# ScalarE's instructions in the order in which the work is given out, and counts widened up to five blocks ahead: a two-layer graph network on one core

## The chip, the cores and the metric

One core of a Trainium2 chip runs the whole program. It has a matmul engine (TensorE, PE in the rows; PEld is its loading of the stationary operand), three engines for elementwise work (VectorE or DVE, ScalarE or ACT, GpSimdE or POOL), an engine that only issues transfers (SyncE or SP), and 16 DMA engines that move data between the main memory and the on-chip memories. Matmul results land in a small memory with banks (tiles whose names end in `_ps`), from which ScalarE or VectorE copies them. Each engine runs its own list of instructions strictly in its order; where an instruction needs another engine's result, it waits, and all that stands behind it on its engine waits with it. The metric is the device time of one execution in microseconds.

## The reference

There are 12500 nodes with 256 features and 200000 edges, sorted by destination. The destinations are drawn as 12500 u^2, so nodes with low numbers have many edges. Two rounds of mean aggregation over the edges, with weights, relu, a last product, the residual and a layer normalisation:

```python
def sage(x, src, dst, W_l, b_l, W_r):
    agg = segment_sum(x[src], dst, num_segments=N_NODES)
    deg = segment_sum(ones(E), dst, num_segments=N_NODES)
    return agg / maximum(deg, 1.0)[:, None] @ W_l + b_l + x @ W_r

h = relu(sage(x, src, dst, W1_l, b1, W1_r))
h = relu(sage(h, src, dst, W2_l, b2, W2_r))
y = x + (h @ W3 + b3)
out = (y - mean(y)) / sqrt(var(y) + 1e-5)      # per node
```

## The kernel before

The nodes lie in 98 blocks of 128 (49 pairs). An aggregation is made in two ways.

*The dense way*, for destinations with low numbers: the edges between every source block and a group of 512 destinations are counted into matrices of 8-bit counts, and the sum over the sources is a product of the source rows with that matrix. `products` runs one such group as a pass over all 98 source blocks. For each block ScalarE casts 128x512 counts to floats (`widened`, line 921, tile `wide`, a pool of WIDE buffers: 5 in layer 1, 7 in layer 2), and TensorE does four matmuls (line 943) into two banks, `dense_ps` and `beside_ps`; the rows come as a rounded part and a rest, which makes two of them per bank. At the end of a pass ScalarE copies the two banks out in four pieces (line 951), and the next pass begins in the same banks. Layer 1 has four passes, layer 2 five. In layer 1 the counts are made beside the passes by `count`: VectorE makes selections (`pick`, line 980), TensorE multiplies them (lines 1005 and 1007) into one of three `count_ps` banks, and ScalarE copies the result as 8-bit numbers to its place (line 1015, at an offset that it loads into a register). Layer 2 reads the counts again, two passes from on-chip memory and three from main memory (the tile `spare`).

*The sparse way*, for the other destinations: a round is four indirect gathers of rows by GpSimdE (line 301, `got`), eight small selection matmuls (line 319) that sum rows by destination into `part_ps` (one bank), a copy to `some` by ScalarE (line 329), and one round later a product with a second selection (`sum_ps`, line 336) that VectorE adds to a ring of sums.

A finished block goes through the weights in pieces. In layer 1 (`first_block`): the product with W_l (line 1181), VectorE's combination (line 1191, `own`), ScalarE's zeroing of the ring's sums (1186) and degrees (1241) and relu (1239). Before, at the start, x @ W_r is made for all blocks (line 877, `splitting`). In layer 2 (`last_block`): transposes copied by ScalarE (1152, `own_t` and `h2_t`, with the relu; a view of the profile writes the latter `h_t`), the products (1179, 1181, 1267), and the normalisation: VectorE's statistics (`mv`, 1273), ScalarE's square root (1275, `std`), VectorE's scaling.

What sets the order: `layer` (line 685) is a generator of work with a plan of costs per engine. It hands out a round of gathers, then block pieces that are due, and fills the rest of a round's time with steps of `products`, `count` and the like. For engines named in `manual_schedule` (line 509: TensorE and GpSimdE) the order of their instructions is the order in which this code gives them out. For the other engines a scheduler, with its own estimate of times, orders the instructions as it sees them become ready. A cast is given out in `products` ahead of a pair of blocks b, b+1, for the blocks up to b+3, where a buffer that it takes may still be in use: it then waits for the products that read it.

Of the kernel before, what the change touches and what calls it, by code (L numbers as in the profile page):

```python
# [20 lines left out]
ACT = mybir.EngineType.Activation  # L21
PE = mybir.EngineType.PE
POOL = mybir.EngineType.Pool
# [8 lines left out]
def kernel(tc, x, src, dst, w1l, b1, w1r, w2l, b2, w2r, w3, b3, out):  # L32

    args = (x, src, dst, w1l, b1, w1r, w2l, b2, w2r, w3, b3, out)  # L40
    with tc.tile_pool(name="flag", bufs=1) as pool:
        flag = pool.tile([1, 1], I32, name="flag")
        by_runs(tc, *args, flag)
        unfit = tc.nc.values_load(
            flag[0:1, 0:1], min_val=0, max_val=1,
            skip_runtime_bounds_check_because="it is clamped to 0..1 where it is made")
    with tc.If(unfit > 0):
        by_sorting(tc, *args)
# [3 lines left out]
def by_runs(  # L52
# [30 lines left out]
    NB = -(-N // P)  # L83
# [267 lines left out]
    with tc.tile_pool(name="setup", bufs=1) as su, \  # L351
# [154 lines left out]
            tc.add_manual_dep(op.ins, first_tables.ins.name, LANDED, reason="the first gathers' tables")  # L506


        ctx.enter_context(tc.manual_schedule(engines={PE, POOL}))
        gathers_1 = Gathers(x, False)  # L510

        def early_round():
# [318 lines left out]
    PAIRS_IN, WIDE = 3, 5  # L831

    def loaded(b, back, table):

        rows = rows_pool.tile([P, 2, 2, D], F32, name="rows", bufs=PAIRS_IN)
        load = nc.sync.dma_start(rows, table[:, b:b + 2])
        freed(load, back)
        if table is h2_d:
            tc.add_manual_dep(load.ins, rows_after, LANDED, reason="the first layer's last gathers")
        return rows  # L840
# [78 lines left out]
    def widened(counted):  # L919
        wide = wide_pool.tile([P, DN], F32, name="wide", bufs=WIDE)  # L920
        nc.scalar.copy(wide.bitcast(F32R), counted)  # L921
        return wide

    def products(n0, counts_of, table, into):


        ps = [pool.tile([P, DN], F32, name=name)
              for pool, name in ((dense_pool, "dense_ps"), (beside_pool, "beside_ps"))]
        rows, counted, wide = {}, {}, {}
        for b in range(0, NB, 2):  # L930
            for u in range(b, min(b + 2 * PAIRS_IN, NB), 2):
                if u not in rows:
                    rows[u] = loaded(u, b - (u - 2 * PAIRS_IN + 1), table)
                    for v in (u, u + 1):
                        counted[v] = counts_of(v)
            for u in range(b, min(b + 4, NB)):
                if u not in wide:
                    wide[u] = widened(counted[u])
            for u in (b, b + 1):
                for k in range(2):  # L940
                    for c in range(NC):
                        own = rows[b][:, u - b, k, c * P:(c + 1) * P].bitcast(F32R)
                        nc.tensor.matmul(ps[c], lhsT=own, rhs=wide[u].bitcast(F32R),  # L943
                                         start=u + k == 0, stop=u == NB - 1 and k == 1)
                used.append(len(strips))
                yield COST_PRODUCT
        assert all(b in given for b in out_of)
        out_of[:] = range(n0 // P, (n0 + DN) // P)
        for i, t in enumerate(into):
            for c in range(NC):  # L950
                nc.scalar.copy(t[:, c], ps[c][:, i * 256:(i + 1) * 256])  # L951
            for j in range(256 // P):
                yield n0 // P + i * (256 // P) + j, t[:, :, j * P:(j + 1) * P]
# [150 lines left out]
    def passed(waiting, n0, counts_of, table, into):  # L1104
        return dense(waiting, products(n0, counts_of, table, into)), NB * max(COST_PRODUCT)
# [190 lines left out]
    PAIRS_IN, WIDE = 4, 7  # L1296
# [389 lines left out]
```

## Time and profile before

| | |
|---|---|
| three runs | 2798.28, 2804.43, 2808.75 us, median 2804.43 |
| profiled execution | 2826.85 us |
| its span | 2824.9 us |
| granted TensorE clock, mean | 0.917 |
| TensorE busy | 2259.9 us, 80% of the span |
| GpSimdE busy | 1775.1 us, 63% |
| VectorE busy | 1296.5 us, 46% |
| ScalarE busy | 1207.0 us, 43% |

Layer 1 takes the stretch from the start to about 1505 us, layer 2 the rest. A row of a group names line, engine, operation, output and inputs with their shape, and how many there are; then its busy time, the mean duration of one in ns, and the engine's idle time just before them with what ended most of it. In a row of waits stand the waiting instruction, the engine and line whose result ended the wait, the sum in us, the count and the longest. A row of the timeline has its start in us, its duration, and in brackets the idle time before it and what ended it; "remote" and "issue" there mean that the profile shows no instruction that ended it. The granted clock is a share of TensorE's full speed.

### The profile page before, as it was taken

The page shows a single profiled execution, that of the slowest core. Times are in us where ns is not written, and L with a number is a line of the kernel's source. Part 1 is how long each engine was busy: PE and PEld are TensorE (multiplying, and loading weights), DVE is VectorE, ACT ScalarE, POOL GpSimd, SP SyncE. Part 2 cuts the span into 40 slices and gives each one's busy share as a digit, 9 for nine tenths or more (in the row PEclk, how much of TensorE's full clock was granted, in tenths as well). Part 3 has the DMA queues.
Part 4 walks back from the last instruction along what each step waited for, and adds up shares of the span by engine and source line. Part 5 has one row for each costly group of instructions (what it writes and reads, how often), then busy time and mean ns, then how long its engine had stood idle before and what let it go on. Part 6 is the DMA issues. An engine that isn't in the chain of part 4 may idle for free.

```text
span 2824.9 us, 42472 instructions
## 1 busy us (share of the span) xinstructions
PE 2259.9 (80%) x12964; PEld 1518.8 (54%) x12964; DVE 1296.5 (46%) x4323; ACT 1207.0 (43%) x2732; POOL 1775.1 (63%) x1812
## 2 busy tenths in 40 slices
PE   3477778888887777788876988888888888888887
PEld 2355555555554455555544556555565665565554
DVE  5655544455556777753463123223223433343345
ACT  0244445665663356654454443333333333333322
POOL 6666666666666666666654666666666666666663
PEclk8688899999998999989988999999998999999998
DMA  5588788779778666677756776777887777767753
GB/s 122 190 277 273 268 280 287 236 236 332 237 228 286 213 211 198 192 238 254 257 168 206 258 236 216 243 239 229 272 262 228 236 249 241 226 204 244 243 156 103
DMA packets 296474, 654.98 MB, mean 232 GB/s; under 512 B 54053, under 2 KB 154351, under 8 KB 296239
## 3 DMA queue, kind: packets, MB, share of 16 engines
q1 hardware_dynamic: 203873, 414.28, 44.5%
q0 software_dynamic: 86496, 236.31, 27.2%
q10 hardware_dynamic: 5870, 1.59, 0.3%
q8 instruction: 108, 1.77, 0.3%
q14 instruction: 127, 1.04, 0.1%
HBM read 542.45 MB, written 109.51 MB: 231 GB/s over the span
## 4 chain that ended last, share of the span: by engine, by line
PE 70%; issue 10%; DVE 6%; another core or an unknown queue 5%; DMA 4%; ACT 3%; POOL 2%; DVEq 0%; ACTq 0%; SPq 0%; POOLq 0%
PE dense_ps L943 14%; PE beside_ps L943 14%; PE part_ps L319 9%; PE block_ps L1181 6%; PE sum_ps L336 5%; PE count_ps L1007 5%; PE dense_ps L877 3%; PE block_ps L1267 3%; PE block_ps L1179 3%; PE block_ps L1150 3%; PE count_ps L1005 2%; POOL got L301 2%; ACT counts L1015 1%; DVE pick L980 1%
## 5 line engine op out<-in xcount | busy, mean ns | idle before, releaser
L301 POOL DMA_INDIRECT got<-in_x_dram,src_t x939 | 950.2, 1012 | 524.5 <-issue 230.6
L301 POOL DMA_INDIRECT got<-h_d,src_t x863 | 823.1, 954 | 490.6 <-issue 229.1
L943 PE MATMUL dense_ps<-wide,rows 128*128 128x512 f32 x1764 | 813.2, 461 | 56.8 <-ACT split L951 17.0
L943 PE MATMUL beside_ps<-wide,rows 128*128 128x512 f32 x1764 | 723.8, 410 | 12.8 <-issue 9.8
L921 ACT CAST wide<-counts 128x512 fp32r<-128x512 uint8 x588 | 352.9, 620 | 332.9 <-PE beside_ps L943 127.9
L943 PEld LDWEIGHTS dense_ps<-wide,rows 128*128 128x128 f32 x1764 | 355.7, 202 | 175.5 <-issue 76.5
L1015 ACT CAST counts<-count_ps 128x343 f32 (+3 forms) x656 | 353.4, 539 | 222.7 <-PE count_ps L1007 104.9
L319 PE MATMUL part_ps<-got,one 128*32 128x257 f32 (+1 forms) x3616 | 336.1, 420 | 75.2 <-issue 31.8
L943 PEld LDWEIGHTS beside_ps<-wide,rows 128*128 128x128 f32 x1764 | 351.3, 199 | 73.0 <-issue 21.7
L980 DVE TENSOR_SCALAR pick<-steps,tables,unit_t 128x343 bf16<-128x343 f16 (+3 forms) x784 | 284.5, 384 | 206.0 <-PE count_ps L1007 98.8
L1007 PE MATMUL count_ps<-pick,low 128*128 128x343 bf16 (+3 forms) x784 | 252.3, 345 | 64.1 <-DVE pick L980 39.6
L921 ACT CAST wide<-spare 128x512 fp32r<-128x512 uint8 x294 | 177.3, 619 | 280.3 <-PE beside_ps L943 99.7
L253 DVE TENSOR_TENSOR one<-lo_t,lane_b 128x128 f32<-128x128 bf16 x452 | 128.5, 286 | 340.2 <-remote 136.2
L349 DVE TENSOR_TENSOR sums<-sums,sum_ps 128x256 f32 x329 | 135.2, 411 | 260.1 <-remote 102.4
L329 ACT COPY some<-part_ps 128x257 f32<-128x257 f32 (+1 forms) x329 | 122.7, 373 | 295.6 <-PE part_ps L319 75.2
L336 PE MATMUL sum_ps<-two,some 128*128 128x128 f32 x1316 | 221.4, 291 | 29.1 <-issue 10.2
L336 PEld LDWEIGHTS sum_ps<-two,some 128*128 128x128 f32 x1316 | 205.8, 204 | 67.0 <-issue 23.0
L1005 PE MATMUL count_ps<-aft,low 128*128 128x49 bf16 x652 | 136.8, 213 | 99.9 <-issue 49.1
L319 PEld LDWEIGHTS part_ps<-got,one 128*32 128x32 f32 x3616 | 81.0, 112 | 247.7 <-issue 185.2
L1007 PEld LDWEIGHTS <-low 128*128 128x128 bf16 x784 | 93.0, 121 | 186.2 <-issue 120.4
L877 PE MATMUL dense_ps<-w1r_sb,own_t 128*128 128x256 f32 x392 | 123.7, 445 | 37.5 <-issue 19.3
L1179 PE MATMUL block_ps<-w2r_sb,own_t 128*128 128x256 f32 x392 | 113.1, 412 | 30.9 <-DVE own L1191 13.3
(204 smaller groups left out, 2448.1 us busy)
## 6 DMA issues: line engine op xcount, KB each, us to landing
rows<-h_d SPq DMA_DIRECT2D x245, 512.0 KB
rows<-x_d SPq DMA_DIRECT2D x196, 512.0 KB
x_d<-counts SPq DMA_DIRECT2D x49, 512.0 KB
h_d<-split SPq DMA_DIRECT2D x98, 256.0 KB
count_d<-counts SPq DMA_DIRECT2D x21, 913.5 KB
spare<-count_d SPq DMA_DIRECT2D x147, 130.5 KB
got<-in_x_dram,src_t POOLq DMA_INDIRECT x939
got<-h_d,src_t POOLq DMA_INDIRECT x863
```

Of the source, the lines that this page charges most:

```text
L301: rows = nc.gpsimd.indirect_dma_start(out=g[:, j, X0:], out_offset=None, in_=self.table, in_offset=bass.IndirectOffsetOnAxis(ap=src_t[:, e ...
L319: strip = nc.tensor.matmul(part_ps[j * W:(j + 1) * W, :width], lhsT=one[:, j], rhs=g[:, row, DW - width:], start=r == 0, stop=r == n - 1)
L336: nc.tensor.matmul(sum_ps[:, c], lhsT=some[:, x0 + c * P:x0 + (c + 1) * P], rhs=two, start=True, stop=True)
L877: nc.tensor.matmul(ps[:, v * D:(v + 1) * D], lhsT=x_t[:, c], rhs=w1r_sb[:, c], start=c == 0, stop=c == NC - 1)
L921: nc.scalar.copy(wide.bitcast(F32R), counted)
L943: nc.tensor.matmul(ps[c], lhsT=own, rhs=wide[u].bitcast(F32R), start=u + k == 0, stop=u == NB - 1 and k == 1)
L980: nc.vector.tensor_scalar(r[:, :w * NP], steps[:, :w * NP], key_t[g][:, t - lo_g:t - lo_g + 1], unit_t[:, t:t + 1], op0=OP.is_equal, op1=O ...
L1005: nc.tensor.matmul(ps[:, :NP], lhsT=before[0], rhs=before[1], start=True, stop=False, skip_group_check=True)
L1007: nc.tensor.matmul(ps[:, :w * NP], lhsT=s, rhs=r[:, :w * NP], start=j == 0 and alone, stop=j == n_in - 1, skip_group_check=not alone)
L1015: copies.append(nc.scalar.copy(to[:, :, bass.ds(off_act.at(t), w)], of).ins)
L1179: nc.tensor.matmul(ps[:, 1], lhsT=own_t[:, c], rhs=wr[:, c], start=c == 0, stop=c == NC - 1)
L1181: product = nc.tensor.matmul(ps[:, 0], lhsT=agg[:, c], rhs=wl[:, c], start=c == 0, stop=c == NC - 1)
```

## The change

ScalarE joins the engines whose order is that of the code. And `products` gives a cast out for the blocks up to b + WIDE - 2, where it was b + 3: in layer 1 (WIDE is 5) that is still b + 3, in layer 2 (WIDE is 7) it is b + 5.

```diff
-        ctx.enter_context(tc.manual_schedule(engines={PE, POOL}))
+        ctx.enter_context(tc.manual_schedule(engines={PE, POOL, ACT}))
...
-            for u in range(b, min(b + 4, NB)):
+            for u in range(b, min(b + WIDE - 1, NB)):
                 if u not in wide:
                     wide[u] = widened(counted[u])
```

TensorE's and GpSimdE's orders are the same before and after. ScalarE's list changes all through; VectorE's and SyncE's, which the scheduler orders in both, change with it. The four loads of the first layer's weights and bias, which ScalarE issues, stood before its first copies to `some` and now stand behind the first five of them.

ScalarE in layer 1, in the second pass. `wide_N` are casts, `counts0_649` the count copies, `some_N` the copy of gathered sums, `ISA` and `TENSOR_LOAD` set the registers for offsets. Numbers tell tiles apart; TensorE uses the wide tiles in the order 8117, 8119, 8157, 8159, 8223, 8225, 8277, 8279. Before:

```order
L1015 COPY counts0_649<-count_ps_8151 128x49x7
L921 CAST wide_8225<-counts1_650 128x512
L329 COPY some_8177<-part_ps_8107 128x257
L240 TENSOR_LOAD spare_105
L1015 ISA
L1015 COPY counts0_649<-count_ps_8180 128x49x7
L921 CAST wide_8277<-counts1_650 128x512
L1186 COPY sums_104<-zero_641 128x2x128
L1015 ISA
L1015 COPY counts0_649<-count_ps_8212 128x49x7
L1239 ACTIVATE own_8065<-own_8065 128x256
```

After:

```order
L1015 COPY counts0_649<-count_ps_8151 128x49x7
L921 CAST wide_8157<-counts1_650 128x512
L921 CAST wide_8159<-counts1_650 128x512
L329 COPY some_8177<-part_ps_8107 128x257
L240 TENSOR_LOAD spare_105
L1015 ISA
L1015 COPY counts0_649<-count_ps_8180 128x49x7
L1186 COPY sums_104<-zero_641 128x2x128
L1239 ACTIVATE own_8065<-own_8065 128x256
L1241 COPY spare_105<-zero_641 1x128
L1015 ISA
L1015 COPY counts0_649<-count_ps_8212 128x49x7
```

The casts now come in pairs, and at the same count copy they are those of two blocks ahead of TensorE (8157 and 8159), where before they were those from 8225 on. The relu (1239) and a zeroing (1241) of a block now stand ahead of a count copy that was ahead of the relu before.

ScalarE in layer 2, round a copy of gathered sums. From here the same tile has another number in the two builds: 22005 before is 22009 after. Before:

```order
L1152 ACTIVATE own_t_21915<-block_ps_21912 128x256
L921 CAST wide_22005<-spare_105 128x512
L921 CAST wide_22007<-spare_105 128x512
L921 CAST wide_22020<-spare_105 128x512
L329 COPY some_21952<-part_ps_17280 128x256
L921 CAST wide_22022<-spare_105 128x512
L1152 ACTIVATE h2_t_21970<-block_ps_21967 128x256
L1186 COPY sums_104<-zero_641 128x2x128
```

After:

```order
L1152 ACTIVATE own_t_21919<-block_ps_21916 128x256
L921 CAST wide_21928<-spare_105 128x512
L921 CAST wide_21930<-spare_105 128x512
L329 COPY some_21956<-part_ps_17280 128x256
L921 CAST wide_21961<-spare_105 128x512
L921 CAST wide_21963<-spare_105 128x512
L1152 ACTIVATE h2_t_21974<-block_ps_21971 128x256
L1186 COPY sums_104<-zero_641 128x2x128
```

The copy has three casts directly ahead of it before and two after, and those after are of earlier blocks: 21928, not 22009.

ScalarE at a change of pass in layer 2. Before:

```order
L921 CAST wide_22368<-spare_105 128x512
L921 CAST wide_22414<-spare_105 128x512
L921 CAST wide_22416<-spare_105 128x512
L951 COPY sums_a_17260<-dense_ps_20367 128x256
L951 COPY sums_a_17260<-beside_ps_20368 128x256
L951 COPY split_648<-dense_ps_20367 128x256
L329 COPY some_22342<-part_ps_17280 128x256
L951 COPY split_648<-beside_ps_20368 128x256
L921 CAST wide_22444<-spare_105 128x512
```

After:

```order
L329 COPY some_22342<-part_ps_17280 128x256
L951 COPY sums_a_17260<-dense_ps_20367 128x256
L951 COPY sums_a_17260<-beside_ps_20368 128x256
L951 COPY split_648<-dense_ps_20367 128x256
L951 COPY split_648<-beside_ps_20368 128x256
L921 CAST wide_22362<-spare_105 128x512
L921 CAST wide_22364<-spare_105 128x512
L921 CAST wide_22366<-spare_105 128x512
L921 CAST wide_22368<-spare_105 128x512
```

The next pass's first casts (22362 and on) stood ahead of the four copies; now they stand behind them.

## The prediction

> **What bounds the kernel now.** I read the page first, then the granted clock by stage, then TensorE's waits in each layer, then ScalarE's groups and, round single waits, the timeline. From the page: the span, the engines' busy time, the chain of work that ended last.
>
> ```profile
> span 2824.9 us, 42472 instructions
> PE 2259.9 (80%) x12964; PEld 1518.8 (54%) x12964; DVE 1296.5 (46%) x4323; ACT 1207.0 (43%) x2732; POOL 1775.1 (63%) x1812
> PE 70%; issue 10%; DVE 6%; another core or an unknown queue 5%; DMA 4%; ACT 3%; POOL 2%; DVEq 0%; ACTq 0%; SPq 0%; POOLq 0%
> ```
>
> TensorE is the bound: 80% busy and 70% of the chain. ScalarE is 43% busy and 3% of the chain, so its order pays only where TensorE stands still for it, and through the clock. Busy time of PE, PEld, DVE, ACT and POOL, granted clock and DMA share: layer 1, layer 2, and layer 2's first pass.
>
> ```profile
> 100.00:1505.00 1405.00, 1114.81 (x6897) 736.39 (x6897) 797.42 (x2771) 747.36 (x1680) 882.53 (x881) 0.92 0.76 246
> 1505.00:2825.00 1320.00, 1115.30 (x5904) 766.09 (x5904) 427.99 (x1321) 456.45 (x1047) 822.14 (x862) 0.93 0.71 226
> 1535.00:1685.00 150.00, 132.76 (x669) 87.16 (x667) 24.29 (x75) 61.12 (x117) 96.67 (x102) 1.00 0.77 254
> ```
>
> TensorE is idle for 290 us of layer 1 and 205 us of layer 2, and the missing clock is worth another 0.08 x 1405 = 112 us and 0.07 x 1320 = 92 us. Roughly, one idle microsecond goes with 0.39 (layer 1) and 0.45 (layer 2) of lost clock. I price a stall's clock by these ratios. TensorE's waits by what ended them (us, count, longest), layer 1:
>
> ```profile
> PE count_ps L1005 <- issue: 49.1, 55, 4.3
> PE count_ps L1007 <- DVE pick L980: 39.6, 20, 22.8
> PE count_ps L1005 <- ACT counts L1015: 35.6, 38, 4.1
> PE dense_ps L943 <- ACT wide L921: 11.4, 3, 9.3
> PE count_ps L1005 <- ACT wide L921: 5.8, 4, 3.0
> ```
>
> and layer 2:
>
> ```profile
> PE part_ps L319 <- ACT some L329: 23.8, 21, 2.7
> PE dense_ps L943 <- ACT split L951: 17.0, 3, 6.6
> PE block_ps L1179 <- DVE own L1191: 13.3, 5, 4.2
> PE block_ps L1181 <- DVE sums L1163: 11.0, 4, 4.3
> PE block_ps L1267 <- ACT h_t L1152: 6.6, 3, 4.3
> PE block_ps L1179 <- ACT wide L921: 3.2, 2, 2.2
> PE dense_ps L943 <- ACT wide L921: 1.7, 2, 1.2
> ```
>
> ScalarE ends 52.8 us of these rows in layer 1 and 52.3 us in layer 2. That is what the change can reach directly.
>
> **The change part by part.** It removes and adds no arithmetic; it fixes the order of these ScalarE groups (busy, mean ns, idle before):
>
> ```profile
> L921 ACT CAST wide<-counts 128x512 fp32r<-128x512 uint8 x588 | 352.9, 620 | 332.9 <-PE beside_ps L943 127.9
> L1015 ACT CAST counts<-count_ps 128x343 f32 (+3 forms) x656 | 353.4, 539 | 222.7 <-PE count_ps L1007 104.9
> L1239 ACT ACTIVATE own<-own 128x256 f32<-128x256 f32 x98 | 41.1, 419 | 19.5 <-DVE own L1191 10.0 <-issue 3.9 <-DVE pick L980 1.4
> L1241 ACT COPY spare<-zero 1x128 f32<-1x128 f32 x82 | 23.8, 290 | 19.5 <-PE count_ps L1005 6.1 <-PE count_ps L1007 4.8 <-PE sum_ps L343 2.2
> ```
>
> *Layer 2, the copies of gathered sums (L329).* Before, the casts run 6 to 7 blocks ahead, each waiting until TensorE frees a wide buffer. The copy stands behind them, and TensorE waits for it, since the next gathered strips go into the one part_ps bank. The casts ahead of the first such stall, and another of the 21 whole:
>
> ```profile
> 1953.63 1.14 ACT L921 CAST wide<-spare 128x512 fp32r<-128x512 uint8 x2 [4.60 <-PE beside_ps L943]
> ...
> 2108.27 0.62 ACT L921 CAST wide<-spare 128x512 fp32r<-128x512 uint8 x1 [2.96 <-PE block_ps L1181]
> 2108.80 0.37 ACT L329 COPY some<-part_ps 128x256 f32<-128x256 f32 x1
> 2109.22 1.08 PE L319 MATMUL part_ps<-got,one 128*32 128x256 f32 x8 [1.39 <-ACT some L329]
> ```
>
> A cast delays what follows by 0.53 us from start to start, so it owns 0.53 of the 1.39 in the last row. Following all 21 stalls so in the timeline, 14 have one cast directly ahead, 6 have two and one has none: 26 x 0.53 = 13.8 us. By the new order the casts ahead of a copy are those of blocks TensorE reaches later anyway, with buffers freed a pair earlier, so they should be done. I take -13, with bounds 0 (the copy waits as long for TensorE's release itself) and -23.8 (the whole row). Clock on these and the next item: 17 x 0.45 = -7.5.
>
> *Other layer-2 waits on ScalarE* (h_t 6.6, wide 3.2 and 1.7, together 11.5): about a third behind casts, as with the copies' half, -4, bounds 0 and -11.5.
>
> The clock rests on short stalls counting. Products start 0.23 us apart before the stall above and 0.43 apart after it:
>
> ```profile
> 2098.55 0.39 PE L943 MATMUL beside_ps<-wide,rows 128*128 128x512 f32 x1
> 2098.78 0.40 PE L943 MATMUL dense_ps<-wide,rows 128*128 128x512 f32 x1
> ...
> 2110.82 0.63 PE L943 MATMUL beside_ps<-wide,rows 128*128 128x512 f32 x1
> 2111.25 0.63 PE L943 MATMUL dense_ps<-wide,rows 128*128 128x512 f32 x1
> ```
>
> The Trainium skill (TensorE: Matmul & The Clock Gate, "HAM oscillation — how this bites in real kernels") says that only gaps in TensorE's work of more than about 3.4 us lose the clock. By that rule the clock terms of this sum (-7.5, -2 and +4) would be nothing and the result about 5 us higher. Here the rule and the trace differ: half speed follows a 1.39 us stall.
>
> *Layer 1, count copies (L1015).* Nine of the 38 stalls of 35.6 us have casts directly ahead of the copy; a cast each and a few doubles come to about 7 us. New casts come in twos in the same queue, so I take -5, bounds 0 and -20; clock 5 x 0.39 = -2.
>
> *Layer 1, relu and zeroing (L1239, L1241)* now stand in the order given out, ahead of the next count copy, where before the scheduler let copies pass. The relu waits for VectorE's own (10.0 us over the whole run), behind it stand the next count copies, and TensorE's counts wait for those. Three count_ps banks cover it: TensorE can fill two more, at 0.345 + 0.213 us a tile,
>
> ```profile
> L1007 PE MATMUL count_ps<-pick,low 128*128 128x343 bf16 (+3 forms) x784 | 252.3, 345 | 64.1 <-DVE pick L980 39.6
> L1005 PE MATMUL count_ps<-aft,low 128*128 128x49 bf16 x652 | 136.8, 213 | 99.9 <-issue 49.1
> ```
>
> so 1.1 us of cover against 0.71 us of work. Without cover it costs 98 x 0.71 = 70 us. Of the two ends the first is nearer: +3.
>
> *Layer 1, the casts' lead.* The wide pool holds 5 here, so the window stays b to b+3, but the scheduler had put casts up to four blocks ahead where the new order gives two. A late cast makes TensorE wait in L943, as in the rows of 11.4 and 5.8 us. Bounds: 0, and half of the 196 pairs late by one cast, 98 x 0.62 = 61 us. I take +7, a bit over half the wait of the nearest rows, since ScalarE is 747 / 1405 = 53% busy; clock for this and the relu +4.
>
> *Pass changes.* The end of layer 2's second pass:
>
> ```profile
> 1909.50 0.37 ACT L951 COPY sums_a<-dense_ps 128x256 f32<-128x256 f32 x1 [0.31 <-issue]
> 1910.92 0.37 ACT L951 COPY sums_a<-beside_ps 128x256 f32<-128x256 f32 x1 [1.05 <-remote]
> 1911.19 0.38 ACT L951 COPY split<-dense_ps 128x256 f32<-128x256 f32 x1
> 1911.46 0.39 ACT L951 COPY split<-beside_ps 128x256 f32<-128x256 f32 x1
> 1911.72 0.64 ACT L921 CAST wide<-spare 128x512 fp32r<-128x512 uint8 x1
> ```
>
> Before, the next pass's first casts stood ahead of these copies, so the first product waited for banks alone (17.0 us in three). Now they stand behind: one copy's pitch of 0.27 and one cast of 0.62 later, 0.9 x 4 = +4. In layer 1 the copies were apart, with a zeroing and a count copy (0.4 and 0.54) between; now they are together: 3 x 0.94, -3.
>
> *At nothing:* the normalisation's std stands ahead of casts and waits for VectorE; the longer lead in layer 2 covers it. The weights' loads move behind the first sums' copies:
>
> ```profile
> 18.54 4.61 ACTq L637 DMA_DIRECT2D w1l_sb<-in_L_gnn_W_l_dram  x1
> 73.73 0.38 ACT L329 COPY some<-part_ps 128x257 f32<-128x257 f32 x1 [3.54 <-PE part_ps L319]
> 104.39 2.07 PE L877 MATMUL dense_ps<-w1r_sb,own_t 128*128 128x256 f32 x4
> ```
>
> from 18.54 to about 74 us with the first use at 104.39; cover gone, their 5 us would show. VectorE's and SyncE's orders, still the scheduler's, change too. Their price is unknown: a third of the VectorE-ended rows (39.6 + 13.3 + 11.0) either way is +-20, and I take 0.
>
> **Sum:** -13 - 7.5 - 4 - 5 - 2 + 3 + 7 + 4 + 4 - 3 = -16.5 us. The profiled execution took 2826.85 us (2 us outside the span), the median of the runs 2804.43, ratio 0.992: (2826.85 - 16.5) x 0.992 = **2788 us**.
>
> **The rivals.** *A, the stalls mostly vanish.* If ScalarE is never behind a cast it cannot start, the whole of L329's 23.8 goes with 11.5 of the other layer-2 rows, and half of layer 1's 52.8: 61.7 us, with clock at 0.42 about 88, less the 15 that the adverse terms cost: -73, 2732. For it: half-speed stretches behind short stalls. Against: nearly half of each wait is TensorE's release and the copy itself.
>
> *B, no change.* TensorE's next operand is late anyway: a saved count copy meets pick (39.6 us), a saved sums copy meets issue or the block's VectorE steps. Gains of 20 shrink to the adverse terms: 2804. For it: ScalarE has 3% of the chain. Against: in the first pass of layer 2 TensorE ran at clock 1.00, so work is there to be taken up.
>
> *C, slower: layer 1's casts come late.* With two blocks of lead, ScalarE must do within a pair of products all it has for that pair: 656 / 196 = 3.3 count copies x 0.539, two casts x 0.620, half a relu and zeroing 0.35, together 3.4 us. TensorE has eight products at 0.23 and 3.3 x 0.558 of counts, 3.7 us. It decides where ScalarE's 3.4, plus any wait for VectorE in its row, passes 3.7. If one pair in four is late by a cast, 49 x 0.62 = 30, with clock 42; with the relu and layer 2's pass changes 49; less half of the gains (34.5 / 2 = 17), +32: 2836. For it: the margin of 0.3 us, and pairs of casts that block count copies. Against: degree and block work adds to TensorE's side.
>
> *D, the order is the scheduler's anyway.* The orders below the change differ throughout, so I give it nothing.
>
> **How the numbers follow.** Chances: the forecast 0.38 (own range 2775 to 2800), A 0.22, B 0.16, C 0.24. About 0.5%, 14 us, is what a measurement here can tell from no change: faster is below 2790, slower above 2818. The forecast lies on the edge; I give 0.25 of it to faster and 0.13 to same. With A, faster is 0.47; with B and 0.02 of C, same is 0.31; slower 0.22. The range, 2722 to 2838, reaches to A's and C's middle and leaves about a tenth outside on each side; it holds the unknown +-20 too.
>
> **What would show it.** Right: L319's wait on L329 in layer 2 at about 10 us and its clock up by 0.01; L951's row near 20 us; L943's wait on L921 in layer 1 at 15 to 25 us. C shows as 40 us or more in that row and a lower clock between 300 and 1400 us, A as ScalarE-ended rows under 50 us in all. A result outside 2775 to 2800 makes the sum wrong; a change that comes from VectorE- or DMA-ended waits makes its reasons wrong.

## The result and the profile after

The changed kernel took 2820.15 us (median of 9 runs, 2808.43 to 2831.12) against 2804.43 for the kernel before (9 runs, 2790.25 to 2809.83). The ratio is **1.007, 95% interval 1.0051 to 1.0089**: slower by 14 to 25 us, where 16 us less was forecast. Its profiled execution took 2831.12 us.

The chips of the experiments have two paces: at the first, as here, the kernel before takes 2799 to 2832 us, at the second 2379 to 2380. So every ratio below is against the kernel before on the same chip, and waits are compared between kernels of one pace.

The page of the changed kernel: span, busy time, chain.

```profile
span 2829.3 us, 42452 instructions
PE 2252.5 (80%) x12964; PEld 1512.9 (53%) x12964; DVE 1299.2 (46%) x4323; ACT 1194.5 (42%) x2732; POOL 1768.4 (63%) x1812
PE 65%; issue 10%; another core or an unknown queue 8%; DVE 6%; ACT 5%; DMA 4%; POOL 1%; ACTq 0%; DVEq 0%; SPq 0%; POOLq 0%
```

The busy times hardly differ. ScalarE's share of the chain rose from 3 to 5%, TensorE's fell from 70 to 65%. The profiled execution of the kernel before was about 20 us over its median, so two spans that differ by 4 us say little here, and the text goes by the waits. TensorE's waits in layer 1 of the changed kernel:

```profile
PE count_ps L1005 <- ACT counts L1015: 38.8, 33, 4.1
PE count_ps L1007 <- DVE pick L980: 37.6, 22, 18.5
PE dense_ps L943 <- ACT wide L921: 25.7, 10, 6.8
PE count_ps L1005 <- issue: 19.9, 32, 2.1
```

and in layer 2:

```profile
PE part_ps L319 <- issue: 38.4, 48, 3.0
PE dense_ps L943 <- ACT wide L921: 24.6, 9, 10.9
PE block_ps L1179 <- ACT own_t L1152: 19.3, 10, 6.0
PE part_ps L319 <- ACT some L329: 12.8, 13, 2.3
PE block_ps L1267 <- ACT h_t L1152: 2.0, 2, 1.2
```

The copies of gathered sums (L329) cost 12.8 us where they cost 23.8, close to the sum's -13. But late casts (L921) stand at 25.7 and 24.6, and own_t at 19.3, where the kernel before has one wait of 1.3. A second profile of this kernel (e5, another chip of this pace) has the casts at 30.9 and 18.2 and own_t at 5.9, so own_t's 19.3 is not a steady size. What stands ahead of own_t is to be seen near the end of the changed kernel, ScalarE first, then TensorE:

```profile
2772.28 0.37 ACT L329 COPY some<-part_ps 128x256 f32<-128x256 f32 x1 [0.76 <-PE part_ps L319]
2775.35 0.29 ACT L1275 ACTIVATE std<-mv,eps 128x1 f32<-128x1 f32 x1 [2.69 <-DVE two L259]
2775.55 0.36 ACT L1152 ACTIVATE own_t<-block_ps 128x256 f32<-128x256 f32 x1
```

```profile
2773.26 0.38 PE L1150 MATMUL block_ps<-ident,own 128*128 128x128 f32 x2
2775.97 2.07 PE L1179 MATMUL block_ps<-w2r_sb,own_t 128*128 128x256 f32 x4 [2.32 <-ACT own_t L1152]
...
2783.13 1.13 PE L1179 MATMUL block_ps<-w2r_sb,own_t 128*128 128x256 f32 x4 [1.17 <-ACT own_t L1152]
```

ScalarE is idle for 2.69 us with std at its head, which waits for VectorE (`two` in the row is VectorE's operation right behind the statistics `mv` that std reads). The copy own_t, of another block, is ready behind it, and TensorE waits 2.32 us for that copy; 7 us later it waits 1.17 us for the next. ScalarE's waits in layer 2 show how general this is, before (first row) and in the changed kernel:

```profile
ACT std L1275 <- DVE mv L1273: 27.6, 28, 2.6
```

```profile
ACT std L1275 <- DVE mv L1273: 84.6, 45, 5.9
ACT std L1275 <- issue: 60.9, 30, 3.2
ACT std L1275 <- DVE z L1269: 29.8, 12, 4.4
```

### The profile page after: what moved, and what is told of

Read it like the earlier page. It is cut to its first block, busy times and chain, and to the rows that moved or that the text cites. A ratio compares the mean times of both kernels' runs of the same rounds, so it can differ in the third digit from the quotient of the medians.

```text
span 2829.3 us, 42452 instructions
## 1 busy us (share of the span) xinstructions
PE 2252.5 (80%) x12964; PEld 1512.9 (53%) x12964; DVE 1299.2 (46%) x4323; ACT 1194.5 (42%) x2732; POOL 1768.4 (63%) x1812
## 4 chain that ended last, share of the span: by engine, by line
PE 65%; issue 10%; another core or an unknown queue 8%; DVE 6%; ACT 5%; DMA 4%; POOL 1%; ACTq 0%; DVEq 0%; SPq 0%; POOLq 0%
PE dense_ps L943 13%; PE beside_ps L943 12%; PE part_ps L319 8%; PE block_ps L1181 6%; PE count_ps L1007 5%; PE sum_ps L336 5%; PE dense_ps L877 3%; PE block_ps L1267 3%; PE block_ps L1150 3%; PE block_ps L1179 3%; PE count_ps L1005 2%; ACT wide L921 1%; ACT counts L1015 1%; POOL got L301 1%
## 5 line engine op out<-in xcount | busy, mean ns | idle before, releaser
L943 PE MATMUL dense_ps<-wide,rows 128*128 128x512 f32 x1764 | 814.1, 462 | 88.4 <-ACT wide L921 50.3
L943 PE MATMUL beside_ps<-wide,rows 128*128 128x512 f32 x1764 | 726.3, 412 | 13.8 <-issue 11.4
L1015 ACT CAST counts<-count_ps 128x343 f32 (+3 forms) x656 | 352.8, 538 | 298.1 <-PE count_ps L1007 99.9
L943 PEld LDWEIGHTS dense_ps<-wide,rows 128*128 128x128 f32 x1764 | 354.4, 201 | 225.8 <-issue 93.2
L319 PE MATMUL part_ps<-got,one 128*32 128x257 f32 (+1 forms) x3616 | 327.2, 417 | 88.4 <-issue 43.3
L943 PEld LDWEIGHTS beside_ps<-wide,rows 128*128 128x128 f32 x1764 | 352.0, 200 | 75.6 <-issue 24.2
L921 ACT CAST wide<-counts 128x512 fp32r<-128x512 uint8 x588 | 332.5, 619 | 49.7 <-remote 23.1
L329 ACT COPY some<-part_ps 128x257 f32<-128x257 f32 (+1 forms) x329 | 123.1, 374 | 532.7 <-remote 190.3
L1007 PE MATMUL count_ps<-pick,low 128*128 128x343 bf16 (+3 forms) x784 | 252.0, 348 | 55.7 <-DVE pick L980 37.6
L319 PEld LDWEIGHTS part_ps<-got,one 128*32 128x32 f32 x3616 | 78.8, 111 | 250.1 <-issue 204.7
L1005 PE MATMUL count_ps<-aft,low 128*128 128x49 bf16 x652 | 136.7, 214 | 73.0 <-ACT counts L1015 39.2
L921 ACT CAST wide<-spare 128x512 fp32r<-128x512 uint8 x294 | 165.0, 620 | 18.7 <-PE beside_ps L943 5.7
L1186 ACT COPY sums<-zero 128x256 f32<-128x256 f32 x160 | 64.8, 405 | 228.1 <-remote 59.0
L877 PE MATMUL dense_ps<-w1r_sb,own_t 128*128 128x256 f32 x392 | 121.5, 438 | 39.3 <-ACT counts L882 18.2
```

The costliest lines, as they stand in the source:

```text
L319: strip = nc.tensor.matmul(part_ps[j * W:(j + 1) * W, :width], lhsT=one[:, j], rhs=g[:, row, DW - width:], start=r == 0, stop=r == n - 1)
L877: nc.tensor.matmul(ps[:, v * D:(v + 1) * D], lhsT=x_t[:, c], rhs=w1r_sb[:, c], start=c == 0, stop=c == NC - 1)
L1005: nc.tensor.matmul(ps[:, :NP], lhsT=before[0], rhs=before[1], start=True, stop=False, skip_group_check=True)
L1007: nc.tensor.matmul(ps[:, :w * NP], lhsT=s, rhs=r[:, :w * NP], start=j == 0 and alone, stop=j == n_in - 1, skip_group_check=not alone)
L1015: copies.append(nc.scalar.copy(to[:, :, bass.ds(off_act.at(t), w)], of).ins)
```

## The experiments

Three theories stood at the outset. *Theory 1*: the fixed order itself costs, by what stands at the head of ScalarE's line (std in layer 2, relu and late casts in layer 1). *Theory 2*: the wider window costs. *Theory 3*: the scheduler, given a ScalarE that it can't arrange, arranges VectorE and SyncE worse.

**Which of the two edits.** The first two runs make one edit each:

```diff
 e1:  manual_schedule(engines={PE, POOL})         # as before
      for u in range(b, min(b + WIDE - 1, NB)):   # as changed
 e2:  manual_schedule(engines={PE, POOL, ACT})    # as changed
      for u in range(b, min(b + 4, NB)):          # as before
```

> Only the second edit (casts given out up to b + WIDE - 2), ScalarE's order left to the scheduler. Theory 1 (the fixed order itself costs, by what stands at the head of ScalarE's line: std waiting for VectorE in layer 2, relu and late casts in layer 1): no change against the kernel before, 2804 us, ratio 0.996 to 1.004, since the scheduler reorders the casts as it did. Theory 2 (the wider window costs: casts of far blocks stand ahead of copies that TensorE needs): the change's whole loss, about 2820, ratio 1.005 to 1.009. Theory 3 (VectorE's and SyncE's shuffled orders cost): in between, as the shuffle goes.

> Only the first edit: ScalarE in the order given out, window b to b+3 in both layers. Theory 1: the change's loss or a little more, 2815 to 2830 us, ratio 1.005 to 1.010, with layer 2's casts given out two blocks ahead and so more of TensorE's waits in L943 for L921 there than the 24.6 us of the changed kernel. Theory 2: the loss is gone, 2804, ratio 0.997 to 1.003.

Measured: e1 1.0004 (0.9991 to 1.0018), e2 1.007 (1.0054 to 1.0085), on a chip where the kernel before takes 2379 us. The order alone makes the loss; the window alone makes none, and Theory 2 falls. TensorE's matmuls stand in one order in all these builds, so a loss can be placed by comparing the same matmul's start. At the matmul between the layers (L1302) e2 is 14.4 us later than e1 (1280.7 against 1266.3), a loss that arises between about 500 and 1000 us; from there to TensorE's last matmul it loses another 9.7 (1106.9 against 1097.2), in the last 60 us. So there are two losses. Their sizes are upper ends: the two profiled executions are 24 us apart, the medians 16. In e3 below, whose first layer is that of e2, the matmul between the layers starts at 1274.7, 8.4 us later than in e1.

The changed kernel with the runs that follow, on a chip of the first pace:

> The changed kernel again, beside the kernel before, so that the runs here have it on their own chip. The edit of e2 alone gave 1.007 and that of e1 1.000, so 1.005 to 1.009, with the loss in two places of the trace if it goes as in e2: between about 500 and 1000 us of layer 1 (some 17 us) and in the last 60 us (8 us).

Measured: 1.0059 (1.0037 to 1.008). The loss is there again.

**Layer 2: std.**

```diff
+        def scaled(n=min(P, N - b * P)):
             std = work.tile([P, 1], F32, name="std")
             nc.scalar.activation(std, mv[:, 1:2], AF.Sqrt, bias=eps)
             ...
+        ends.append(scaled)      # run at the start of the next call of pieces()
```

> The changed kernel, but layer 2's std, and what follows it of a block, is given out half a round later, so ScalarE no longer meets it while VectorE's statistics are still being made. Theory 1: TensorE's waits for own_t (19.3 us, of these 8 of 10 with std directly ahead) and for std (2 us) fall under 6 us, and with their clock the time falls by 20 to 28: 2792 to 2802 us, ratio 0.996 to 1.000. Theories 2 and 3: no change from the changed kernel, 2815 to 2825, ratio 1.005 to 1.009.

Measured: 1.0021 (1.001 to 1.0032), against 1.007 for e2 on the same chip. That is less of a gain than was expected: 0.21% is left. TensorE's waits in layer 2, e2 first, then e3:

```profile
PE block_ps L1179 <- ACT own_t L1152: 12.0, 9, 2.1
PE dense_ps L943 <- ACT wide L921: 7.4, 5, 2.2
```

```profile
PE dense_ps L943 <- ACT wide L921: 7.5, 5, 2.2
```

The wait for own_t is gone and nothing took its place; from the matmul between the layers to the last e3 takes 1097.3 us, as e1 does. e3 has the wider window too, which e2 has not; but e4 below, with the wider window and with std as the change has it, takes 1109.5 us for that stretch. So on this chip std at the head of ScalarE's line cost about 10 us. At the first pace this is not so plain (e17 and e18 below).

**Layer 1: relu.** The same edit on `first_block`: relu, the zeroing of degrees and the stores go to `ends`.

> The changed kernel, but layer 1's relu, the zeroing of its degrees and the stores behind it are given out half a round later. Theory 1: of the count copies' 38.8 us the stalls with relu and zeroing directly ahead (12 of 33, about 14 us) go, with clock 15 to 20: 2800 to 2808 us, ratio 0.998 to 1.002. If relu only passes its wait on to the next copy, or its blocks become late for the ring of sums: 2815 to 2825. Theories 2 and 3: 2815 to 2825.

Measured: 1.0081 (1.0066 to 1.0097), no better than e2. The count copies did get through: TensorE's wait for them in layer 1 (L1005 on L1015) was 17.5 us in e2 and is 7.4 here. But relu frees own's buffer, by way of its store, and the next block's own is loaded into that. The rows of waits of e1, then of e4, in layer 1: SyncE's to issue that load, VectorE's for the load, and TensorE's for the rows that SyncE loads too:

```profile
SPq L1209 <- DMA h_d<-own: 87.6, 64, 3.7
DVE own L1231 <- DMA own<-xw_d: 89.2, 45, 4.7
PE dense_ps L943 <- DMA rows<-x_d: 8.6, 6, 3.4
```

```profile
SPq L1209 <- DMA h_d<-own: 118.3, 65, 4.1
DVE own L1231 <- DMA own<-xw_d: 121.7, 63, 7.3
PE dense_ps L943 <- DMA rows<-x_d: 15.1, 9, 4.1
```

All three are larger than in e1. But e2, with relu as the change has it, has 100.2, 140.0 and 17.6 us: against it only SyncE's wait grew. So giving relu out later is no cure, what took back the 10 us of the count copies is not shown, and VectorE's wait, which is large in both, is the trail to follow.

**VectorE's order by itself.** ScalarE goes back to the scheduler. Instead, VectorE's operations are tied one behind the other, by dependencies that set only the order, as e2 has them:

```diff
+    for a, b in zip(order, order[1:]):        # order: a table of 4315 numbers
+        tc.add_manual_dep(tape[b], tape[a].name, IN_ORDER, reason="held order")
```

ScalarE's order then differs little from that before (in e6 162 of its 2732 instructions stand elsewhere, by 5 places at most); e7 ties SyncE's transfers as well.

> The kernel before, with only VectorE's order changed: its 4315 operations are chained in the order that the scheduler gives them in e2, while ScalarE and SyncE are left to the scheduler and stand almost as before. Theory 1 (ScalarE's own line makes the loss): no change, 0.998 to 1.002. Theory 3 (the scheduler, given a ScalarE that it can't arrange, arranges VectorE worse, as the wait of own's addition for its load suggests, 28.6 us in e1 and 47.4 in e2 over the stretch of the loss): layer 1's part of the loss comes with it, 1.004 to 1.006, and the last 60 us stay as before.

> As e6, with SyncE's order that of e2 as well. Theory 1: 0.998 to 1.002. Theory 3 with the loads' order in it (TensorE's wait for rows was 3.5 us in e1 and 10.0 in e2 over the stretch of the loss): 1.004 to 1.007, and more than e6.

Measured: e6 1.008 (1.0056 to 1.0105), e7 1.0037 (1.002 to 1.0054). VectorE's order alone can carry a loss as large as the whole, though ScalarE stands nearly as before. Against the expectation e7 loses less than e6: with the order of SyncE that was made beside it VectorE's order costs some 0.37%, 10 us, and this is the better size for its part in the changed kernel, where both stand so. No run ties VectorE's operations in the order of before, so what the tying costs by itself is not told apart from the order. The two orders of VectorE differ almost only in layer 1. Of the lines that repeat, the one that moves most there is L1231, the addition of the bias to own, by 5.6 places on the average: 34 of its 98 stand earlier, by up to 29 places, 25 later, by up to 26, and 39 where they were. The next two runs split the shuffle at that line: e9 moves only the 98 additions of L1231, e10 all the others.

> The kernel before, with only VectorE's order changed, and of that only the 98 additions of layer 1's bias to own (L1231): each stands where it stands in e2, all other operations keep the order of before. Theory 3a (this addition, which waits for own's load, moved ahead of selections that TensorE needs, makes layer 1's loss): 1.003 to 1.008 as in e6. Theory 3b (the loss comes from the rest of the shuffle, pick, one and the sums' additions): 0.998 to 1.002.

> The other half of e9: VectorE's order is that of e2, but the 98 additions of L1231 stand where the kernel before has them. Theory 3a: 0.998 to 1.002. Theory 3b: 1.003 to 1.008.

Measured: e9 1.0103 (1.0081 to 1.0126), e10 1.0037 (1.0019 to 1.0056). The 98 additions alone lose most, and all the others still lose 0.37%: e9 lies above the range of theory 3a, e10 in that of 3b, so neither theory is the whole (ScalarE and the loads were left to the scheduler). VectorE's wait for the load and TensorE's wait for pick in layer 1, in e1, e9 and e10 (chips of the second pace; with a held order VectorE's operations are given out through a helper and carry its line, L1705):

```profile
DVE own L1231 <- DMA own<-xw_d: 89.2, 45, 4.7
PE count_ps L1007 <- DVE pick L980: 18.0, 24, 3.7
```

```profile
DVE own L1705 <- DMA own<-xw_d: 157.4, 60, 11.2
PE count_ps L1007 <- DVE pick L1705: 47.5, 39, 7.7
```

```profile
DVE own L1705 <- DMA own<-xw_d: 96.1, 47, 5.5
PE count_ps L1007 <- DVE pick L1705: 12.8, 21, 2.5
```

In e9 the addition holds VectorE for 68 us more, the selections (pick) are late, and TensorE waits 29.5 us more for them. In the fixed order itself this path is weaker: e2 has 140.0 us of the first wait, but only 21.6 of the second. And at the first pace, that of the forecast, the first wait is small and hardly moves, in the kernel before, then in the changed one:

```profile
DVE own L1231 <- DMA own<-xw_d: 14.3, 10, 3.4
```

```profile
DVE own L1231 <- DMA own<-xw_d: 22.0, 14, 3.2
```

In e5 it is 9.9, and TensorE's wait for pick goes from 39.6 to 37.6 (43.0 in e5). So that the addition makes the loss of the changed kernel at the first pace is not shown; the tied kernels e6 and e7 have 46.6 and 31.9 us of that wait there.

**Both cures.** Std as in e3, and the bias added after the product:

```diff
-        nc.vector.tensor_add(own, own, biases[:, 0])
         yield 0.22, 0.4, 0.0
         ...
         h = sage(None, b, agg, since, w1l_sb, None, None, own)
+        nc.vector.tensor_add(h, h, biases[:, 0])
```

> The changed kernel with std given out half a round later (as e3), and with the bias added after the product with W_l instead of before it, so that VectorE no longer meets own's load early in its line. Theory 1 for layer 2 and theory 3a for layer 1: both losses go, 0.996 to 1.000. Theory 3b: layer 1's part stays, 1.002 to 1.004.

Measured: 0.9979 (0.9967 to 0.9991), beside e9 and e10. The loss is gone on this chip, and the kernel is a little faster than before. What the later addition does to the scheduler's order at this pace was not run, so how much of this cures the new order, and how much any order would gain, stays open. The opposite way, VectorE also in the order given out (std as in e3, the bias added where it was):

```diff
-        ctx.enter_context(tc.manual_schedule(engines={PE, POOL, ACT}))
+        ctx.enter_context(tc.manual_schedule(engines={PE, POOL, ACT, DVE}))
```

> As e3, and VectorE too in the order in which the code gives the work out, so that nothing on TensorE, ScalarE, GpSimdE or VectorE is left to the scheduler. If layer 1's loss is the scheduler's bad guess for VectorE once ScalarE is fixed, the code's order need not have it: 0.996 to 1.001 (e3 had 1.002). If VectorE's operations, given out at once after the products that they wait for, block the selections behind them: 1.005 or more.

Measured: 1.0667 (1.0641 to 1.0693). VectorE then waits, with its additions to the ring of sums, for the product just given out, and TensorE for the selections behind:

```profile
DVE sums L349 <- PE sum_ps L336: 285.5, 68, 15.7
PE count_ps L1007 <- DVE pick L980: 117.7, 112, 7.6
PE count_ps L1007 <- DVE low L970: 74.9, 39, 34.5
```

**Is the fixed order worth anything once cured?** On a chip of the first pace, the two cures on the kernel before (e13 the addition alone, e14 both), and on the changed one (e15, the kernel of e11):

> The kernel before (ScalarE by the scheduler) with the bias added to own after the product with W_l. If own's addition also cost the kernel before its waits (89.2 us of VectorE in e1), 0.994 to 0.998; if it only hurts where the scheduler has moved it, 0.999 to 1.002.

> The kernel before with both cures of e11 and nothing else. If ScalarE's fixed order is worth the 10 to 20 us that the prediction's sum gave it, this is slower than e15 by 0.3 to 0.7%; if the order is worth nothing by itself, it is within 0.2% of e15; if the scheduler's order is the better one, faster than e15 by 0.2% or more.

> The kernel of e11 again, beside e13 and e14 on their chip: 0.996 to 1.000.

Measured: e13 0.9995 (0.9975 to 1.0014), e14 1.0001 (0.9989 to 1.0014), e15 **1.0042** (1.0027 to 1.0058). The cures are worth nothing to the scheduler's order, and at this pace the fixed order still loses 0.4% with them; e11's gain does not carry over. The wait that grew most is in layer 1, e14 first, then e15:

```profile
PE dense_ps L943 <- ACT wide L921: 3.0, 1, 3.0
```

```profile
PE dense_ps L943 <- ACT wide L921: 28.5, 14, 8.8
```

These are the late casts. Two runs give layer 1's casts out one by one, four blocks ahead instead of two at once: e8 on the changed kernel, e16 on that of e15.

```diff
-            for u in range(b, min(b + WIDE - 1, NB)):
-                if u not in wide:
-                    wide[u] = widened(counted[u])
             for u in (b, b + 1):
+                for v in range(u, min(u + (WIDE if WIDE == 5 else WIDE - 1 - u % 2), NB)):
+                    if v not in wide and v in counted:
+                        wide[v] = widened(counted[v])
```

> The changed kernel, but in layer 1 a cast is given out for the block four ahead just before each block's products, not for two blocks at once two to three ahead. Theory 1 with late casts: TensorE's wait in L943 for L921 in layer 1 falls to a half or less and the time by 4 to 10 us, ratio 1.003 to 1.005. If the casts, now each behind a buffer just freed, hold up the count copies instead: 1.007 or more.

> The kernel of e11 with layer 1's casts given out singly, four blocks ahead (the edit of e8). Late casts cost TensorE 9.6 us of waits in layer 1 of e11: 0.001 to 0.004 under e15 if they are late for want of lead, the same as e15 or worse if the casts then hold up count copies.

Measured: e8 1.0051 (1.0029 to 1.0073) beside 1.0059 for e5; e16 1.0028 (1.0013 to 1.0043) beside 1.0042 for e15. The wait of e16:

```profile
PE dense_ps L943 <- ACT wide L921: 9.7, 2, 8.4
```

It fell from 28.5 to 9.7 us, and the medians by 3.6 us; from e5 to e8 it fell from 30.9 to 15.1. The intervals overlap in both pairs, so the wait is shown to be one of lead, and a gain in time is not shown. With these waits and both cures e16 still loses 0.28%; what that is made of stays open.

**Layer 2 alone.** ScalarE's order fixed only from layer 2 on, e18 with std later:

```diff
+    ctx.enter_context(tc.manual_schedule(engines={PE, POOL, ACT}))
     gathers_2 = Gathers(h_d, True)
```

> ScalarE's order fixed from the second layer's start on, with the window of the changed kernel; layer 1 stays the scheduler's as before. The copies' gain (11 us in the profile, with clock 13 to 17) against std's loss at the end (8 to 10 us): 0.996 to 1.001. If the copies' gain is not there in time: 1.003 to 1.005.

> As e17, with std given out half a round later. If the prediction's layer-2 terms hold (-13, -4 and -7.5 of clock, +4 for pass changes): 0.991 to 0.996. If the fixed order gains nothing in layer 2 but only does not lose: 0.998 to 1.001.

Measured: e17 1.0000 (0.9977 to 1.0024), e18 0.9996 (0.9977 to 1.0015). So at this pace all that the change does in layer 2, std at the head included, costs and gains nothing that can be seen, and the loss of 0.6 to 0.7% needs layer 1. Between e17 and e18, which differ by std alone, the medians are 0.5 us apart; the profiles take 1318.7 and 1314.3 us from the matmul between the layers to the last, so a cost of some us is possible, and one of 10 is not shown. In e18 the wait for the copies is 15.1 us (in e17, where std holds ScalarE, it is 30.3): the copies' gain is in the waits and not in the time. Where it went is best read in e14 and e15, with both cures, on one chip, layer 2. Scheduler's order (e14):

```profile
PE part_ps L319 <- ACT some L329: 32.4, 24, 3.5
PE dense_ps L943 <- issue: 11.5, 22, 1.7
PE dense_ps L943 <- ACT split L951: 10.9, 3, 5.7
PE block_ps L1179 <- DVE own L1191: 10.0, 4, 4.6
PE block_ps L1181 <- DVE sums L1163: 5.3, 3, 2.9
```

Fixed order (e15):

```profile
PE part_ps L319 <- ACT some L329: 15.0, 16, 3.0
PE dense_ps L943 <- issue: 18.8, 26, 4.6
PE dense_ps L943 <- ACT wide L921: 10.5, 4, 7.1
PE block_ps L1179 <- DVE own L1191: 17.3, 5, 4.7
PE block_ps L1181 <- DVE sums L1163: 13.8, 4, 5.3
```

The copies give 17.4 us back. The pass changes wait for the cast (10.5) where they waited for the copies out (10.9), which is nearly even. TensorE then stands 7.3 us longer for "issue" at the products, 7.3 longer for own, and 13.8 for sums, where e14 has 5.3. All rows of the layer add up to 197 us in e14 and 198 in e15. What stands behind "issue" the profile doesn't show, so a part stays open.

## Why the prediction was wrong

Split by layers, the sum is -20.5 us for layer 2 (-13, -7.5, -4 and +4) and +4 for layer 1. Layer 2 alone measured 0.0 us (e17, -6.5 to +6.8) and -1 (e18, -6.5 to +4). So of the 32 us between 2788 and 2820 some 20 are layer 2's, where the sum promised a gain that did not come, and some 12 are layer 1's. Step by step, by the sum's terms:

- **Copies of gathered sums, -13, and the clock on them, -7.5:** right as a wait, 23.8 to 12.8 in the profile of the change and 32.4 to 15.0 between e14 and e15. Wrong as time: e18 has these terms and std out of the way, and is at 0.9996, where they promised 0.993. The step that failed is the one from a wait to the span. The prediction took a saved stall as saved whole, with 0.45 of clock on top; rival B said that the next operand would be late anyway, and for layer 2 that is what the runs show.
- **"At nothing: the normalisation's std stands ahead of casts and waits for VectorE; the longer lead in layer 2 covers it":** this step failed at the second pace. It named the casts behind std and not the transposed copies. own_t of another block stands there too, TensorE needs that at once, and in the tail there are no casts. It was priced at 0 and is about 10 us there (layer 2 takes 1106.9 us in e2 and 1109.5 in e4, and 1097.3 in e3). At the pace of the forecast the stall is in the trace, but e17 and e18 show no such cost in time.
- **"VectorE's and SyncE's orders ... +-20, and I take 0":** the price was called unknown and its middle was taken, and that is not borne out. VectorE's order, tied, gave 1.008 at the first pace in e6 (22 us) and, with SyncE's, 1.0037 in e7 (10 us); the 98 additions of L1231 alone gave 1.0103 at the second pace in e9. So the price can reach the whole loss. What it is in the changed kernel stays open, since the wait of the addition hardly moves there, and with that addition later e15 still loses 0.42%.
- **Casts' lead in layer 1, +7:** the mechanism was right and the size was off. The row went from 11.4 to 25.7 in the change (+14.3; 30.9 in e5), and from 3.0 to 28.5 between e14 and e15, which have the same cures. e16 with four blocks of lead shows 9.7. How much of it is time is not shown.
- **Count copies, -5, and relu, +3:** the count copies' row went from 35.6 to 38.8 us, +3.2 for the two together where -2 was taken; e5 has 31.8, so the sign is not settled. The price of relu left out that relu's store frees the buffer of the next own; e4, with relu later, gained nothing.
- **Other layer-2 waits, -4:** h_t went from 6.6 to 2.0, as forecast, and own_t took it back (19.3, and 5.9 in e5).
- **Pass changes, +4 in layer 2:** right in kind. The first products of the passes wait for a cast now, no longer for banks; the row of L943 for L921 in layer 2 (24.6) stands where L951's 17.0 and L921's 1.7 stood, +5.9.

So the failed step that is shown at the pace of the forecast is the first; which step of layer 1 made the loss is not settled. The signs that the prediction gave for being right were signs of waits, and two of the four came close to true (L319 at 12.8, layer 1's casts at 25.7) while the time went the other way.

Of the rivals, B (2804) and C (2836) lie equally far from 2820. C named the late casts, but its sign of 40 us in that row was not reached, so it is not shown. The clock terms (-7.5, -2, +4) cannot be told apart from the scatter: the granted clock was 0.917 in the profile before and 0.919 after, and in layer 2 it went from 0.93 to 0.94, but e14, with the scheduler's order, has 0.94 too. The pair of L1179 rows above bears on how the clock is lost: four matmuls took 2.07 us after the wait of 2.32 us, and 1.13 us after that of 1.17. So half speed again followed a gap that is shorter than the 3.4 us of the Trainium skill (TensorE: Matmul & The Clock Gate, "HAM oscillation — how this bites in real kernels"), though not every short gap, and the trace does not agree with that rule as a threshold.

## What to carry to other kernels

When one engine's order is fixed by hand and others stay with a scheduler, compare the other engines' orders too, and look first for operations that wait for a load or for a long chain: on an engine that takes its list in order each can be a gate for all that is behind it, whatever it costs itself. Giving such an operation out later, where its input is long there, was worth 10 us for std at one pace and nothing measurable at the other, so try a cure where the loss was measured. And count a removed wait as time only after asking what the waiting engine meets next; here 17 us of waits were worth nothing.

## What the runs showed of the hardware

The same program runs 15% apart on the chips of the two paces (2804 and 2379 us). In the profiles of the kernel before (first pace) and of e1 (second pace), VectorE is busy for 1297 and 1309 us and GpSimdE for 1775 and 1767. TensorE's busy time goes from 2259.9 to 2077.5 us, with the granted clock at 0.917 and 0.963; that is 182 of the 452 us between the two spans, and the other 270 are its idle time. The chain that ended last, 70% TensorE at the first pace, is another in e1:

```profile
PE 39%; DMA 25%; POOL 18%; issue 10%; DVE 5%; ACT 1%; DVEq 0%; ACTq 0%; SPq 0%; POOLq 0%
```

So the two paces test the change against different limits. The group of one of the counting matmuls, the kernel before at the first pace, then e1, in whose layer 1 nothing is changed, at the second:

```profile
L1005 PE MATMUL count_ps<-aft,low 128*128 128x49 bf16 x652 | 136.8, 213 | 99.9 <-issue 49.1
```

```profile
L1005 PE MATMUL count_ps<-aft,low 128*128 128x49 bf16 x652 | 134.5, 213 | 15.5 <-ACT counts L1015 11.7
```

One instruction takes 213 ns on both; the idle time before them is 99.9 us on one and 15.5 on the other. That a handover between engines costs more at the first pace would fit this, and would fit a fixed order that gains 0.2% at the second pace (e11) and loses 0.4% at the first (e15), but no run shows it. Why the chips differ was not found.
